# Another order, bank plan and loading of the first windows in a fused window-attention and Fourier kernel

## The chip, the cores and the metric

The kernel runs on one core of one Trainium2 chip. The metric is device time in microseconds (us) of one execution. The engines are TensorE (PE, which multiplies matrices and loads its weights ahead as PEld), VectorE (DVE), ScalarE (ACT), GpSimd (POOL) and SyncE (SP, which issues transfers here). Each engine works through its own queue in order. [...]

## The reference

There are 32 images of 56 x 56 positions and 128 channels, and two residual layers.

```python
x = x + window_attention(group_norm(x))   # 7x7 windows, shifted by 3, 4 heads of 32
x = x + fourier(group_norm(x))            # 32 groups of 4 channels in both norms

# window_attention, per window of 49 tokens
attn = q @ k.T * 32 ** -0.5 + bias + mask         # relative position bias, shift mask
out  = softmax(attn) @ v @ w_proj.T + b_proj

# fourier: the first 32 DCT modes along w and along h, mixed over channels, turned back, added
h   = idct(mix(dct(x, w)[:32], w0)) + idct(mix(dct(x, h)[:32], w1))
out = relu(h @ W1 + b1) @ W2 + b2                 # 128 -> 512 -> 128
```

## The kernel before, in words

All is computed in fp32. The work is written out in cycles by hand, with PE, ACT, DVE and POOL bound to the order of the program text (`manual_schedule`, L1073); SP's queue is ordered by the framework. Cycle r is one row of eight windows: image r // 8, row r % 8. A row passes through a pipeline of cycles:

- cycle r: `attn_qk` (L393): the products Q and K on PE, one bank each; ACT empties Q once and K twice, one time for each of two heads (L406, L416). `attn_scores` (L438): 16 products of K with Q into two banks (L451), emptied by DVE, which adds bias and mask `bm` (L459). `attn_max` (L466): DVE takes the maximum (L469), POOL subtracts it (L470). `attn_v` (L424): the product V (L429), copied by ACT (L436).
- the exponential on ACT (L476), the sum and its inverse on DVE (L481, L483), then POOL divides by multiplication in six pieces, into `blocks` (L495).
- cycle r + 2: DVE turns `blocks` (L505).
- cycle r + 3: `attn_values` (L508): probabilities times V into two banks (L520), emptied by ACT (L552) and DVE (L550). `attn_project` (L554): the output product, to which DVE adds the input with its bias, giving x (L569).
- cycle r + 4: sums of x and of its square over channels (L586, L593 on ACT, L594).

In the first eleven cycles (`CONV_BEGIN` is 11) `first_rows` (L1031) orders this: Q and K, the exponential of the row before, values, token bias on POOL, the division of the row before, turn, scores, maximum and subtraction, projection, steps of the norm of the next image, V. Two score buffers `a_sb` alternate. From cycle 11 on other functions (L894 to L1020) order it, and the Fourier layer of the image that is through runs beside the attention: statistics (`fourier_stats`, L608), transforms (L666), mixing (L700), going back (`modes_back`, L739, emptied by ACT L755 or DVE L750), and from cycle 19 the feed-forward in seven of eight cycles (`ff_in`, L759: four hidden blocks, each product into a bank, emptied by ACT at L776; `ff_out`, L790, emptied by DVE at L811). All `halved` products carry the line L110.

The banks are handed out in turn from two rings of four, and a product waits until the bank four places back in its ring has been emptied:

```python
def attn_bank(): return bank("pa", 4)   # Q, K, values, scores, V, projection, statistics, norm
def conv_bank(): return bank("pc", 4)   # transforms, mixing, modes, feed-forward
```

Loading and normalizing an image: its rows come in two halves k of 32 rows and two quarters u of each (`load_quarter`, L136), one buffer; DVE turns a quarter so that channels come on partitions (`turn_quarter`, L296: L308 to L319), takes statistics of each row (L329), and `image_norm` (L336) goes in steps from those to the power on POOL (rstd, L377), the scaled weights on ACT (wn, L385) and V's bias (L388, L389). Image 0 is loaded in two halves, four transfers each, from SP and ACT (L146). The relative position bias is set up by seven transfers of columns (L180), seven of rows (L184) and one copy (L187), the mask by four (L195), and `bias_and_mask` (L201) adds the two: for inner rows on DVE ahead of the cycles, for the last row of an image on POOL in cycles 4 and 5. POOL's memset in `mix_weights` (L244) precedes each load of a part of the mixing weights.

## Time and profile before

| | before |
|---|---|
| time, median of 3 runs | 3379.4 us (3378.18 to 3388.73) |
| time of the profiled execution | 3378.94 us |
| span in the profile | 3377.1 us |
| PE busy | 3252.4 us (96%) |
| weight loads (PEld) | 2561.5 us (76%) |
| DVE busy | 2468.8 us (73%) |
| POOL busy | 2334.6 us (69%) |
| ACT busy | 1979.1 us (59%) |
| moved by DMA | 448.85 MB, 133 GB/s on average |

The profile is one execution, as the hardware's profiler took it. Its page gives the busy time of each engine, its busy tenths in 40 equal slices of the span, and the clock that the throttle granted PE, in tenths. Views of the trace give busy time by stretches, the instructions in order of time (start, duration, engine, line, output <- inputs, and in brackets how long the engine had stood and what ended that), and who waited for whom. Ends of matmuls are modelled, since they are pipelined: rows overlap by a few tenths of a us.

### The profile page before, as it was taken

The page shows a single profiled execution, that of the slowest core. Times are in us where ns is not written, and L with a number is a line of the kernel's source. Part 1 is how long each engine was busy: PE and PEld are TensorE (multiplying, and loading weights), DVE is VectorE, ACT ScalarE, POOL GpSimd, SP SyncE. Part 2 cuts the span into 40 slices and gives each one's busy share as a digit, 9 for nine tenths or more (in the row PEclk, how much of TensorE's full clock was granted, in tenths as well). Part 3 has the DMA queues.
Part 4 walks back from the last instruction along what each step waited for, and adds up shares of the span by engine and source line. Part 5 has one row for each costly group of instructions (what it writes and reads, how often), then busy time and mean ns, then how long its engine had stood idle before and what let it go on. Part 6 is the DMA issues. An engine that isn't in the chain of part 4 may idle for free.

```text
span 3377.1 us, 158257 instructions
## 1 busy us (share of the span) xinstructions
PE 3252.4 (96%) x69504; PEld 2561.5 (76%) x69504; DVE 2468.8 (73%) x4793; ACT 1979.1 (59%) x3649; POOL 2334.6 (69%) x2724
## 2 busy tenths in 40 slices
PE   4689999999999999999999999999999999999999
PEld 2467777777878777777777777777777777777776
DVE  6778777777777777777778777777777778777641
ACT  2456665566655666666666665566665666665553
POOL 5777777677676777777777676677776777777641
PEclk8889999999999999999999999999999999999999
DMA  5546555556555555555556555555555655555443
GB/s 94 111 117 149 134 132 139 130 136 147 131 132 132 141 133 142 140 133 137 137 137 147 134 133 131 135 135 141 135 139 134 140 137 140 138 135 132 117 129 101
DMA packets 1158097, 448.85 MB, mean 133 GB/s; under 512 B 509951, under 2 KB 1127584, under 8 KB 1157408
## 3 DMA queue, kind: packets, MB, share of 16 engines
q1 hardware_dynamic: 1149565, 437.50, 54.2%
q8 instruction: 546, 8.95, 1.2%
q10 hardware_dynamic: 7843, 1.24, 0.3%
q14 instruction: 143, 1.17, 0.1%
HBM read 277.01 MB, written 161.48 MB: 130 GB/s over the span
## 4 chain that ended last, share of the span: by engine, by line
PE 78%; DVE 8%; POOL 5%; ACT 5%; issue 3%; DMA 1%; SPq 0%; DVEq 0%; POOLq 0%; ACTq 0%
PE pc L110 36%; PE pa L110 13%; PE pa L429 6%; PE pc L666 5%; PE pc L739 5%; PE pa L451 5%; PE pa L520 4%; PE pc L700 4%; POOL blocks L495 4%; ACT hid L776 2%; POOL a L470 1%; DVE eT L505 1%; DVE a L459 1%; DVE xw L308 1%; DVE st L329 1%
## 5 line engine op out<-in xcount | busy, mean ns | idle before, releaser
L495 POOL TENSOR_TENSOR blocks<-a,rs 32x512 f32<-32x512 f32 (+3 forms) x1536 | 1304.3, 856 | 646.9 <-DVE rs L483 542.4
L110 PE MATMUL pc<-wff,hid 128*64 128x128 f32 x12544 | 744.2, 273 | 2.5 <-issue 1.0
L110 PE MATMUL pc<-xf,wff 128*64 128x512 f32 (+2 forms) x3584 | 720.1, 539 | 1.1 <-DVE xf L750 0.9
L110 PEld LDWEIGHTS pc<-wff,hid 128*64 128x64 f32 x12544 | 705.0, 137 | 10.5 <-ACT hid L776 4.6
L110 PEld LDWEIGHTS pc<-xf,wff 128*64 128x64 f32 x3584 | 291.4, 136 | 344.1 <-issue 229.7
L470 POOL TENSOR_TENSOR a<-a,mx 128x784 f32<-128x784 f32 x256 | 386.0, 1508 | 235.4 <-DVE mx L469 202.5
L776 ACT ACTIVATE hid<-pc,b1sb 128x512 f32<-128x512 f32 (+2 forms) x896 | 512.9, 646 | 60.7 <-PE pc L110 52.6
L550 DVE TENSOR_SCALAR oT<-pa,bqkv 128x147 f32<-128x147 f32 (+2 forms) x768 | 171.1, 279 | 376.1 <-PE pa L520 376.1
L593 ACT ACTIVATE xr<-x 112x384 f32<-112x384 f32 (+1 forms) x256 | 147.1, 574 | 509.5 <-DVE x L569 509.5
L110 PE MATMUL pa<-xw,wn 128*64 128x392 f32 x2048 | 400.8, 500 | 41.3 <-ACT wn L385 36.2
L811 DVE TENSOR_TENSOR res<-pc,res 128x512 f32<-128x512 f32 (+3 forms) x257 | 143.0, 566 | 373.6 <-issue 168.3
L436 ACT COPY v<-pa 128x512 f32<-128x512 f32 x256 | 152.1, 594 | 356.4 <-PE pa L429 356.1
L783 POOL TENSOR_TENSOR res<-res,b2sb 128x512 f32<-128x512 f32 (+2 forms) x256 | 266.8, 1048 | 88.2 <-DMA res<-scr 88.2
L416 ACT ACTIVATE k<-pa,bqkv,heads 128x392 f32<-128x392 f32 x512 | 317.5, 673 | 2.3 <-PE pa L110 1.9
L476 ACT ACTIVATE a<-a 128x784 f32<-128x784 f32 x256 | 218.8, 855 | 170.4 <-POOL a L470 160.4
L505 DVE STREAM_TRANSPOSE eT<-blocks 128x1024 f32<-128x1024 f32 x256 | 315.7, 1233 | 0.0
L429 PE MATMUL pa<-wn,xw 128*64 128x128 f32 x4096 | 290.1, 283 | 15.9 <-issue 7.8
L124 POOL TENSOR_TENSOR xr<-xr,bproj 112x384 f32<-112x384 f32 (+1 forms) x256 | 292.5, 1142 | 7.4 <-DMA xr<-in_x_dram 7.3
L459 DVE TENSOR_TENSOR a<-pa,bm 128x392 f32<-128x392 f32 x512 | 265.2, 560 | 30.1 <-PE pa L451 6.5
L520 PEld LDWEIGHTS pa<-eT,v 49*32 49x32 f32 x16384 | 173.7, 106 | 146.5 <-issue 94.7
L110 PE MATMUL pa<-wproj,oT 128*48 128x128 f32 (+1 forms) x3584 | 253.3, 276 | 21.7 <-ACT oT L552 15.4
L481 DVE TENSOR_REDUCE sm<-a 128x16 f32<-128x784 f32 x256 | 245.2, 958 | 35.6 <-ACT a L476 35.5
(94 smaller groups left out, 5023.0 us busy)
## 6 DMA issues: line engine op xcount, KB each, us to landing
zscr<-z SPq DMA_DIRECT2D x512, 112.0 KB
xin<-in_x_dram SPq DMA_DIRECT2D x496, 112.0 KB
htok<-scr SPq DMA_DIRECT2D x256, 196.0 KB
zT<-zscr SPq DMA_DIRECT2D x192, 256.0 KB
res<-scr SPq DMA_DIRECT2D x160, 256.0 KB
out_dram<-res SPq DMA_DIRECT2D x160, 256.0 KB
scr<-x SPq DMA_DIRECT2D x128, 224.0 KB
xr<-in_x_dram SPq DMA_DIRECT2D x128, 168.0 KB
```

What stands on the lines that cost most here:

```text
L110: nc.tensor.matmul(dst[ps], lhsT=lhsT[:, ps], rhs=rhs, start=start, stop=stop)
L124: nc.gpsimd.tensor_tensor(piece, piece, bproj.unsqueeze(1).to_broadcast([TC, n, C]), ALU.add)
L416: nc.scalar.activation(k_sb[:, u], pk[:, :RT].rearrange("p (w j) -> p w j", j=WT), AF.Identity, bias=im.bias[:, 3 + u : 4 + u], scale=head ...
L429: nc.tensor.matmul(pv[HALVES[w % 2], w // 2 * C : (w // 2 + 1) * C], lhsT=im.half[i // NP][:, t0 : t0 + JP], rhs=im.w[:, 2 * C : 3 * C], s ...
L459: nc.vector.tensor_tensor(a[:, 2 * hp : 2 * hp + 2, :, 0:WT].rearrange("p u w j -> p w u j"), ps[hp][:, :RT].rearrange("p (w u j) -> p w u ...
L470: nc.gpsimd.tensor_tensor(a3, a3, mx.unsqueeze(2).to_broadcast([P, 2 * NWR, WT]), ALU.subtract)
L481: nc.vector.tensor_reduce(sm, a3, axis=AX.X, op=ALU.add)
L495: nc.gpsimd.tensor_tensor(dst[to, k, :, :n], a3[src, :, kb * KB : kb * KB + n], rs[src].unsqueeze(2).to_broadcast([src.stop - src.start, 2 ...
L505: nc.vector.transpose(eT.rearrange("p t (k j) -> p k t j", k=2), blocks[r % 2])
L520: nc.tensor.matmul(po4[u][h * HD : (h + 1) * HD, pr], lhsT=v[ks, pr, h * HD : (h + 1) * HD], rhs=eT[ks, h * NP + pr, :WT], start=True, sto ...
L776: nc.scalar.activation(hf[:, :n], ph[:, :n], AF.Relu, bias=b1sb[:, f : f + 1])
L783: nc.gpsimd.tensor_tensor(im.res[:m, c0:c1], im.res[:m, c0:c1], b2sb[:m].unsqueeze(1).to_broadcast([m, c1 - c0, C]), ALU.add,)
```

## The change

Seven things change together.

1. Banks: `pa` has two (Q, K, values, V). The scores have two banks of their own, `ps0` and `ps1`, zeroed once by DVE. The projection, V's bias and the statistics take banks of `pc`, which has four as before.
2. Scores: the weights are the 49 columns of a window and no longer 64, and only 49 of each 64 partitions are written. `q_sb` loses its padding.
3. The first rows use three score buffers, the third in a buffer of the transforms' y, which is free then.
4. In `first_rows` the values come ahead of the scores, as before, but scores, maximum, subtraction and exponential of a row now all stand ahead of the division of the row before.
5. Image 0 is loaded in quarters, 16 transfers of half the size, alternately from SP and ACT.
6. The 19 transfers of bias and mask are issued by POOL. The bias sums come behind the first norm on DVE, those of the last row in cycles 1 and 2 on DVE.
7. Two of the three norm steps of cycle 7 move to the end of cycle 6. The zeroing of the ends of xw goes from POOL to DVE.

```diff
     def attn_bank():
-        return bank("pa", 4)
+        return bank("pa", 2)
...
+    ps = [bank(f"ps{hp}", 1) for hp in range(2)]
+    for t in ps:
+        nc.vector.memset(t, 0.0)
...
-        pb = attn_bank()
+        pb = conv_bank()
...
-                        ps[hp][HALVES[e], pr * 2 * WT : (pr + 1) * 2 * WT],
-                        lhsT=q[cs, w * WT : w * WT + JP],
+                        ps[hp][e * JP : e * JP + WT, pr * 2 * WT : (pr + 1) * 2 * WT],
+                        lhsT=q[cs, w * WT : (w + 1) * WT],
...
-        pp = attn_bank()
+        pp = conv_bank()
...
-        pg = attn_bank()
+        pg = conv_bank()
...
+    def attn_buffer(r):
+        return a_sb[r % 3 if r < CONV_BEGIN - 2 else r % 2]
...
-            (nc.scalar if ix % 2 else nc.sync).dma_start(
+            nc.gpsimd.dma_start(
                 cols[ix : ix + 1].rearrange("p h y x -> p (h y) x"), src.unsqueeze(0)
             )
         for iy in range(WS):
-            nc.sync.dma_start(
+            nc.gpsimd.dma_start(
...
-    nc.sync.dma_start(rpb[JP : JP + WT], rpb[0:WT])
+    nc.gpsimd.dma_start(rpb[JP : JP + WT], rpb[0:WT])
...
-            nc.sync.dma_start(mask_sb[rows, :, k], src.rearrange("r p j -> p r j"))
+            nc.gpsimd.dma_start(mask_sb[rows, :, k], src.rearrange("r p j -> p r j"))
...
+            queue = nc.scalar if b == 0 and cb % 2 else nc.sync
+            queue.dma_start(t[cs], x[b, rows, u * HW : (u + 1) * HW, cs])
...
     def first_rows(cycle):
         im, i = row(cycle)
+        im3, i3 = row(cycle - 3)
         if im:
             attn_qk(im, i)
-        if cycle:
-            attn_exp(cycle - 1)
-        im3, i3 = row(cycle - 3)
         if im3:
             attn_values(im3, i3, cycle - 3)
         tokens_bias(cycle)
-        divide(cycle)
-        turn(cycle)
         if im:
             attn_scores(im, i, cycle)
             attn_max(cycle)
+            attn_exp(cycle)
+        divide(cycle)
+        turn(cycle)
         if im3:
             attn_project(im3, i3)
-        for _ in range(3 if cycle == NWR - 1 else cycle in (0, NWR)):
+        for _ in range(cycle in (0, NWR - 1, NWR)):
             norm_step(cycle)
...
-        if cycle in (4, 5):
+        if cycle in (1, 2):
             for half in range(2):
-                bias_and_mask(nc.gpsimd, 1, cycle - 4, half)
+                bias_and_mask(nc.vector, 1, cycle - 1, half)
         next_begin(cycle)
         next_groups(cycle)
+        if cycle == NWR - 2:
+            for _ in range(2):
+                norm_step(NWR - 1)
...
         if cycle == CONV_BEGIN - 1:
             attn_sums(im3, i3)
-            attn_exp(cycle)
...
+        extra = big.tile([P, NM * S + JP - S], F32, tag="y", name="a_extra", bufs=2)
+        extra = extra[:, : NH * NP * WT].rearrange("p (t w j) -> p t w j", t=NH, w=NP)
+        a_sb.append(extra)
```

More of the change, by code (lines that the diff above doesn't have):

```diff
@@ L128, in swin_fourier_kernel, with load_quarter @@
     HW = S // 2
-    def load_columns_of(dst, b, k, w0, w1, both=False):
+    def load_quarter(b, k, u):
+        if b:
+            t = work.tile([P, HW, KB], F32, tag="xin", name="xin", bufs=1)
+        elif u:
+            t = others[k]
+        else:
+            t = big.tile([P, NM * S + JP - S], F32, tag="y", name="xin_first", bufs=2)
+            t = t[:, : S * KB].rearrange("p (w c) -> p w c", w=S)
+            others.append(t[:, HW:])
+            t = t[:, :HW]
         rows = slice(k * (S - KB), k * (S - KB) + KB)
@@ L133, in load_columns_of @@
             cs = slice(cb * KB, (cb + 1) * KB)
-            (nc.scalar if both and cb % 2 else nc.sync).dma_start(dst[cs], x[b, rows, w0:w1, cs])
-    def load_quarter(b, k, u):
-        t = work.tile([P, HW, KB], F32, tag="xin", name="xin", bufs=1)
-        load_columns_of(t, b, k, u * HW, (u + 1) * HW)
+            queue = nc.scalar if b == 0 and cb % 2 else nc.sync
+            queue.dma_start(t[cs], x[b, rows, u * HW : (u + 1) * HW, cs])
         return t
-    xins = {}
+    xins, others = {}, []
     for k in range(2):
-        first = big.tile([P, NM * S + JP - S], F32, tag="y", name="xin_first", bufs=2)
-        first = first[:, : S * KB].rearrange("p (w c) -> p w c", w=S)
-        load_columns_of(first, 0, k, 0, S, True)
         for u in range(2):
-            xins[0, k, u] = first[:, u * HW : (u + 1) * HW]
+            xins[0, k, u] = load_quarter(0, k, u)
     x1 = big.tile([TC, NCH, C], F32, tag="x1", name="x1")
@@ L210, in bias_and_mask @@
                 )
-    for t in range(2):
-        for half in range(2):
-            bias_and_mask(nc.vector, 0, t, half)
     dct_w = const_load([TC, 2 * NM], dct, "dct_w")
@@ L271, in swin_fourier_kernel @@
         nc.vector.memset(heads[h * HD : (h + 1) * HD, h % 2 : h % 2 + 1], 1.0)
-    q_sb = big.tile([P, RT + JP - WT], F32, tag="q", name="q")
-    nc.gpsimd.memset(q_sb, 0.0)
+    q_sb = big.tile([P, RT], F32, tag="q", name="q")
     v_sb = [big.tile([P, NP, C], F32, tag=f"v{i}", name=f"v{i}") for i in range(3)]
     a_sb = [big.tile([P, NH, NP, WT], F32, tag=f"a{i}", name=f"a{i}") for i in range(2)]
+    def attn_buffer(r):
+        return a_sb[r % 3 if r < CONV_BEGIN - 2 else r % 2]
     blocks = [
@@ L302, in turn_quarter @@
             )
-            nc.gpsimd.memset(im.half[k][:, NWR * slot : NWR * slot + JP - WT], 0.0)
+            nc.vector.memset(im.half[k][:, NWR * slot : NWR * slot + JP - WT], 0.0)
         slots = im.half[k][:, : NWR * slot].rearrange("p (j h s) -> p s j h", j=NWR, s=WS)
@@ L438, in attn_scores @@
     def attn_scores(im, i, r):
-        q, a = q_sb, a_sb[r % 2]
-        ps = [attn_bank(), attn_bank()]
+        q, a = q_sb, attn_buffer(r)
         for pr in range(NP):
@@ L466, in attn_max @@
     def attn_max(r):
-        a3 = a_sb[r % 2].rearrange("p t w j -> p (t w) j")
+        a3 = attn_buffer(r).rearrange("p t w j -> p (t w) j")
         mx = small.tile([P, 2 * NWR], F32, tag="mx", name="mx")
@@ L474, in attn_exp @@
     def attn_exp(r):
-        a2 = a_sb[r % 2].rearrange("p t w j -> p (t w j)")
+        a2 = attn_buffer(r).rearrange("p t w j -> p (t w j)")
         nc.scalar.activation(a2, a2, AF.Exp)
     def attn_recip(r):
-        a3 = a_sb[r % 2].rearrange("p t w j -> p (t w) j")
+        a3 = attn_buffer(r).rearrange("p t w j -> p (t w) j")
         sm = small.tile([P, 2 * NWR], F32, tag="sm", name="sm")
@@ L486, in attn_divide @@
     def attn_divide(r, rs):
-        a3 = a_sb[r % 2].rearrange("p t w j -> p (t w) j")
+        a3 = attn_buffer(r).rearrange("p t w j -> p (t w) j")
         dst = blocks[r % 2]
@@ L1081, in swin_fourier_kernel @@
             norm_step(-1)
+        for t in range(2):
+            for half in range(2):
+                bias_and_mask(nc.vector, 0, t, half)
+        extra = big.tile([P, NM * S + JP - S], F32, tag="y", name="a_extra", bufs=2)
+        extra = extra[:, : NH * NP * WT].rearrange("p (t w j) -> p t w j", t=NH, w=NP)
+        a_sb.append(extra)
         for cycle in range(NB * NWR + CONV_BEGIN + FF_AT[-1] - NWR + 1):
```

## The prediction

> **What bounds the kernel now.** I read the page's busy lines and slices first, then busy time by stretches, then the order of time and the waits of three stretches: the first rows (0 to 149 us), the cycles before the feed-forward starts (149 to 235 us), and one later image.

> ```profile
> PE   4689999999999999999999999999999999999999
> PEclk8889999999999999999999999999999999999999
> ```

> A slice is 84.4 us. PE fills from the fourth slice on; only the first three have room.

> ```profile
> 100.00:120.00 20.00, 10.27 (x228) 6.34 (x224) 14.79 (x33) 7.78 (x16) 12.60 (x17) 0.80 0.44 71
> ...
> 2440.00:2840.00 400.00, 398.85 (x8648) 311.32 (x8644) 308.51 (x596) 245.97 (x456) 289.17 (x333) 1.00 0.57 137
> ```

> Columns: stretch, us, then busy us of PE, weight loads, DVE, ACT, POOL, the clock, the DMA share. Late in the run PE is busy 398.85 of 400 us at clock 1.00: there any wait put in front of PE is paid in full, and nothing that the other engines save is. From 0 to 240 us PE is busy 148 us, so 92 idle us are all that the change can win. In the first rows this chain sets the pace:

> ```profile
> 43.58 1.50 POOL L470 TENSOR_TENSOR a<-a,mx 128x784 f32<-128x784 f32 x1
> ...
> 45.11 0.86 ACT L476 ACTIVATE a<-a 128x784 f32<-128x784 f32 x1 [4.39 <-POOL a L470]
> ...
> 46.00 0.97 DVE L481 TENSOR_REDUCE sm<-a 128x16 f32<-128x784 f32 x1 [4.35 <-ACT a L476]
> ...
> 47.40 5.33 POOL L495 TENSOR_TENSOR blocks<-a,rs 128x512 f32<-128x512 f32 x6 [2.27 <-DVE rs L483]
> ...
> 52.81 1.50 POOL L470 TENSOR_TENSOR a<-a,mx 128x784 f32<-128x784 f32 x1
> ```

> Subtraction, exponential, sum, division, next subtraction: 52.81 - 43.58 = 9.23 us a cycle. The score additions (L459) of cycles 0 to 10 start at 31.39 and 133.93, so ten cycles take 102.54 us; two of them are long. Cycle 5 to 6 takes 14.27, with the load of a quarter waited for, and 7 to 8 takes 15.86, since the second image's scaled weights come last:

> ```profile
> 84.09 1.10 DVE L308 STREAM_TRANSPOSE xw<-xin 128x512 f32<-128x512 f32 x1 [4.38 <-DMA xin<-in_x_dram]
> ```

> ```profile
> 107.56 1.57 PE L110 MATMUL pa<-xw,wn 128*64 128x392 f32 x4 [6.83 <-ACT wn L385]
> ```

> **The change, part by part.** The sum is made against the profiled execution, 3378.94 us (span 3377.1 and 1.84 around it), 0.5 below the median of 3379.4. A cycle takes in one row of eight windows.

> *Start: +1 us.* Image 0 in quarters lets DVE's turns begin earlier. They began at 9.97, when 0.9 MB had landed, and DVE was then busy to 20.95. One quarter's turns (2.1 us) go ahead of that; the last quarter is still followed by turns, a copy and four statistics (2.0 + 0.2 + 2.0), so about 0.8 us is won. Against it, 19 small transfers go from SP and ACT to POOL: seven columns, four masks, seven rows, one copy, each kind waiting for an earlier one. They stand ahead of the power (rstd, L377, at 23.58), for which ACT's weights and PE wait. The trace has no transfer issued by POOL. Issued by SP the same ones took 1.18 each for columns (4.70 for 4), 0.45 (masks), 0.83 (rows), 0.80: 16.7 in all, and the copy landed 3.4 us after its issue began. From 2.1 (the memset of bm) that gives columns to 10.4, masks to 13, rows to 19, landing, copy at 22.2: hidden. At the dearest issue in the trace, 2.07 each (8.27 for four quarters' loads), 19 take 39 us and the power comes some 19 us late. I take +1, near the transfers' own rows, and keep -1 to +19. The bias sums on DVE (16 at 0.18) end by 29, two us ahead of the first scores. [...]

> *First rows: -3 us.* With the subtraction ahead of the division the 9.23 us chain is cut: exponential and sum lie beside the division. POOL then needs 1.50 + 5.33 + 1.13 (token bias) + 0.4 = 8.4. But a longer loop takes its place, since the exponential of a cycle now stands in ACT's queue ahead of the copy of V, the bank of that copy is the one that the next product for K needs (two banks left), and the product of probabilities and V needs K's bank: subtraction 1.50, exponential 0.86, square 0.56, copy of V 0.58, product K 0.78, evictions 1.25, values 0.95, scores 0.90, additions 1.00, maximum 0.97, less some 0.2 of overlap and with handovers of 0.05: 9.5. So an ordinary cycle gains nothing. The first two have no values and no square: 8.0 each; the third and fourth 9.0. Cycle 5 to 6: the sums of biases leave POOL, so the weights' memset and the quarter's load behind it on SP come earlier; DVE's own work (10.6) and the landing leave 11.4. Cycle 7 to 8: two steps of the norm go ahead; the weights are ready, and mean products and their evictions add 0.9 to 10.1: 11.0. Sum 8 + 8 + 9 + 9 + 10 + 11.4 + 9.5 + 11 + 9.5 + 9.5 = 94.9, 7.6 less. At the end POOL has two divisions to make one after the other: from the additions of cycle 10 to the end of its division, 2.0 (additions, maximum) + 1.5 + 5.4 + 1.4 (sums, token bias) + 5.4 = 15.7, where 147.62 - 133.93 = 13.7 were taken; 5.6 of the gain is left. The clock takes part of it: PE now stands 2.1 to 3.1 us in front of product K, on the loop. In this trace a stop of 2.06 us (at 176.29) was followed by scores of 1.58 instead of 0.90, one of 1.77 (122.75) by full speed. That is 1.4 us a cycle, 0 to 14 in all; I take 2.6. Bounds -7 to +9. [...]

> *Cycles 11 to 18: +7 us.* With four banks the values could run while ACT was still evicting K; with two they stand behind it. Cycle 17 of before:

> ```profile
> 210.23 0.92 PE L520 MATMUL pa<-eT,v 49*32 49x49 f32 x62 [1.90 <-DVE x L569]
> ...
> 211.08 2.52 PE L739 MATMUL pc<-idcth,zT 64*64 64x112 f32 x48
> ...
> 211.22 1.24 ACT L416 ACTIVATE k<-pa,bqkv,heads 128x392 f32<-128x392 f32 x2
> ...
> 213.37 1.10 PE L451 MATMUL pa<-k,q 64*64 64x98 f32 x32
> ...
> 214.52 0.57 DVE L459 TENSOR_TENSOR a<-pa,bm 128x392 f32<-128x392 f32 x1 [1.48 <-PE pa L451]
> ```

> Values began at 210.23 as soon as x was out; K's evictions ended at 212.46. Values, the modes and the scores behind them on PE go 2.2 later, and DVE was waiting for those scores. About +2.0 here, +2.05 in cycle 18 (values 220.06, K out 222.17). In cycle 14 the scores waited for K anyway (178.46); values now stand between: +0.85. In cycle 11 V's product waited for DVE (149.16); its bank will be the one that ACT empties behind four copies of y (151.24): +2.1. The wait of values for x (5.9 us in three cycles) goes, but x is ahead of K in ACT's queue (square, Q, K), so K is late next. Bounds 0 to +8.

> *All later images: +10 us.* PE is the bound. Banks of the scores and the bank of the projection change no wait there: K is out 0.09 to 1.9 us ahead of the values in every cycle that I read. But the statistics of image b (L613) take a bank of the feed-forward's four, right behind the four hidden blocks, so the bank of the first, which ACT must have emptied:

> ```profile
> 431.45 1.24 ACT L416 ACTIVATE k<-pa,bqkv,heads 128x392 f32<-128x392 f32 x2
> ...
> 432.57 2.43 ACT L776 ACTIVATE hid<-pc,b1sb 128x512 f32<-128x512 f32 x4
> 432.69 0.29 PE L110 MATMUL pa<-tot,gmean 112*64 112x64 f32 x4
> ```

> The first of the four blocks is out at 432.57 + 0.65 = 433.22, PE is there at 432.69: 0.55 of waiting. Over 30 images this time is 0.45 to 0.57 in 18, and 0 to 0.3 in the rest: 10.5 us. Bounds 0 to 11. The lone wait of values in the cycle without feed-forward has 0.09 to spare: up to 1.5, in the bounds.

> *Narrower score weights: -1.* 49 columns instead of 64. The scores take 0.72 us from start to start in a late image, and their moving columns are the same; weight loads of 64 columns (137 ns) and of 32 (106) bound it at 0 to -5. PE's stops for no visible reason (L429, L666, L739; 22 us between 340 and 3200) may fall elsewhere: -6 to +6.

> Sum: 1 - 3 + 7 + 10.5 - 1 = +14.5, so **3393 us**.

> **The rivals.** *Faster, 0.15:* POOL becomes the bound of the first rows. If the copy of V is out early, so that product K follows product Q at once, ten cycles are 8.4 to 11 each, 87 us instead of 102.5; with 2 lost at the end, start -1, and the later waits covered (ACT a little earlier than before), that is some -15: 3364. For it: the 9.23 us chain is really cut. Against it: ACT's order puts the copy behind the exponential in every cycle. It decides from the point where the loop through ACT falls under 8.4.

> *No change, 0.20:* the wait of the statistics is hidden because their own input is late as well (DVE's part ends at 432.70). Then +4: 3383.

> *Much slower, 0.10:* POOL's transfers cost 2.07 each and hold the power: +18 on top, 3411. For it: 19 issues in one queue, four links of waiting. Against: POOL has stood idle from 4.6 to 23.6.

> *The forecast, 0.55:* 3385 to 3403, with the terms above; some four fifths of it lie above 3389.

> **The numbers.** 0.3% is 10 us, about what a measurement of this kernel can tell from no change; its borders are 3369 and 3389. Slower: 0.44 of the forecast and the 0.10 of the transfers, 0.54. Faster: 0.15, and 0.01 from the low end of the second case. Within: 0.11 of the forecast and 0.19, 0.30. The range leaves out about half of the faster case and half of the slowest: 3366 to 3408.

> **What would show it.** In the profile after: ordinary first cycles of 9 to 10 us with PE's second product waiting for the copy of V; no wait of PE for wn near cycle 8; a wait for K ahead of the values in cycles 14, 17 and 18; a wait of about 0.5 us at the product of tot, once an image; the power within 2 us of 23.6. First cycles of 8.4 us, or no wait at tot, would make the forecast wrong.

## The result and the profile after

| | before | after |
|---|---|---|
| time, median of 6 runs each, same chip | 3379.76 us (3374.62 to 3388.73) | 3423.75 us (3417.15 to 3433.5) |
| after / before | | 1.0129, 95% interval 1.0109 to 1.0148 |
| span of the profiled execution | 3377.1 us | 3431.7 us |
| PE busy | 3252.4 us | 3273.1 us |

The change costs 44 us. The forecast had the sign, but 13 of 44 us, and the time lies above its range (3366 to 3408). The profiled execution of after is the slowest of its six: its span is 54.6 us longer, so some 10 of what the traces compare below are scatter. Two of six runs of the kernel with the bank part alone, and one of six of the kernel with the statistics' sums in a scores' bank, took 7.6 to 9.5 ms; the times given for these two are medians of their other runs.

First the slices of the page, then two of the stretches shown of before (same columns):

```profile
PE   4679999999999999999999999999999999999999
PEclk8789999999999999999999999999999999999999
```

```profile
2440.00:2840.00 400.00, 386.44 (x8369) 301.43 (x8367) 294.90 (x579) 236.45 (x438) 279.61 (x318) 1.00 0.55 133
100.00:120.00 20.00, 14.54 (x270) 10.96 (x272) 15.14 (x36) 7.50 (x16) 14.73 (x22) 0.67 0.54 106
```

The slices look alike. The stretches do not: late in the run PE is busy 386.44 of 400 us where it was busy 398.85, at clock 1.00, and from 100 to 120 us its clock is 0.67 where it was 0.80.

**Where the time goes.** I compared the start of the same instruction in both traces. After starts its first score additions 0.9 us earlier (30.52). At cycle 10 it is 2.9 us late, at cycle 11 4.8, at the first product of `tot` of image 1 (242.95 against 231.30) 11.7, and from there it loses on, to 54 at image 30: some 43 us in the later images.

**The first rows** run in the loop that the forecast described. One cycle in order of time:

```profile
96.95 1.50 POOL L476 TENSOR_TENSOR a<-a,mx 128x784 f32<-128x784 f32 x1 [2.62 <-DVE mx L475]
...
98.49 0.86 ACT L482 ACTIVATE a<-a 128x784 f32<-128x784 f32 x1 [4.72 <-POOL a L476]
...
99.66 0.57 ACT L443 COPY v<-pa 128x512 f32<-128x512 f32 x1
...
100.28 0.89 PE L110 MATMUL pa<-xw,wn 128*64 128x392 f32 x4 [2.13 <-ACT v L443]
...
102.58 0.80 PE L526 MATMUL pa<-eT,v 49*32 49x49 f32 x62 [1.21 <-ACT k L423]
...
103.30 1.56 PE L457 MATMUL ps<-k,q 64*49 64x98 f32 x32
```

The exponential (L482) waits for the subtraction, the copy of V (L443) stands behind it, PE's product for K waits 2.13 us for that copy's bank, and the values wait for K's eviction. The scores then take 1.56 us instead of 0.90: PE is cold, by which I mean the granted clock, 0.50 from 103.30 to 104.80 where it was 1.00 at K's product (100.28 to 101.17). Cycles take 9.6, 9.6, 11.1, 9.5, 9.4, 15.1, 10.7, 11.5, 9.5, 10.4, in all 106.3.

**The later images.** What PE waited for between 340 and 3200 us (total us, times, longest), after first, then before:

```profile
PE pc L745 <- issue: 22.8, 18, 2.2
PE pc L672 <- issue: 14.5, 16, 2.1
PE pa L436 <- issue: 9.4, 10, 1.5
PE pc L110 <- POOL blocks L501: 7.4, 15, 0.5
PE pc L110 <- issue: 1.9, 4, 0.6
```

```profile
PE pc L666 <- issue: 8.2, 14, 1.1
PE pa L429 <- issue: 7.8, 10, 1.6
PE pc L739 <- issue: 6.1, 7, 1.4
...
PE pc L110 <- issue: 1.0, 3, 0.4
```

The fourth line of after is the wait at `tot` that the forecast named; in order of time:

```profile
446.62 2.43 ACT L782 ACTIVATE hid<-pc,b1sb 128x512 f32<-128x512 f32 x4
...
447.45 0.34 PE L110 MATMUL pc<-tot,gmean 112*64 112x64 f32 x4 [0.49 <-POOL blocks L501]
```

The first of the four hidden blocks is out at 446.62 + 0.65 = 447.27, and `tot` follows; the view names POOL, whose event came at about the same time, but the bank is ACT's. That is 7.4 us. The rest is "issue": stops in which PE waited for nothing that the profile shows. They grow from 23.1 to 48.6 us.

**What an "issue" stop is.** Part 3 of the page of after (queue, kind: packets, MB, share) has a queue that moves instructions:

```profile
q8 instruction: 546, 8.95, 1.2%
```

```profile
1373.21 0.34 PE L110 MATMUL pc<-tot,gmean 112*64 112x64 f32 x4 [0.54 <-POOL blocks L501]
...
1373.59 0.81 PE L526 MATMUL pa<-eT,v 49*32 49x49 f32 x64
1374.33 0.89 PE L457 MATMUL ps<-k,q 64*49 64x98 f32 x32
1375.04 0.93 PE L745 MATMUL pc<-idctw,zT 64*64 64x112 f32 x28
1377.92 0.79 PE L745 MATMUL pc<-idctw,zT 64*64 64x112 f32 x20 [1.95 <-issue]
```

The packet with the next piece starts at 1375.41, takes 0.88 us, and PE goes on 1.63 us after its end. Over the 82 borders of before that come under 5 us behind the one ahead and at which PE goes on within 1.9 us of the packet's end, the packet starts 1.5 us after PE has crossed the border ahead (median), takes 1.1, and is used 1.5 later: 4.1 us for a piece. More than half of the pieces last PE 5 to 9 us (267 of 481 of before between 340 and 3200 us), and nothing shows. But from `tot` on PE has 64 products for the values, 32 for the scores and 48 for the modes, in the trace each with a weight load of its own: a whole piece in 2.4 us.

An image has 4373 instructions in before and 4370 in after, 17 pieces and 21 or 18 more. So the borders move through the program from image to image and are back after 12 to 14: before's images take 100.2 us where the borders fall into sparse stretches and up to 103.4 where they fall behind the dense ones.

### The profile page after: what moved, and what is told of

The parts are those of the page before. It is cut to its first block, busy times and chain, and to the rows that moved or that the text cites. A ratio compares the mean times of both kernels' runs of the same rounds, so it can differ in the third digit from the quotient of the medians.

```text
span 3431.7 us, 158187 instructions
## 1 busy us (share of the span) xinstructions
PE 3273.1 (95%) x69504; PEld 2565.1 (75%) x69504; DVE 2481.5 (72%) x4875; ACT 1978.7 (58%) x3649; POOL 2335.5 (68%) x2662
## 3 DMA queue, kind: packets, MB, share of 16 engines
q10 hardware_dynamic: 7712, 1.24, 0.3%
## 4 chain that ended last, share of the span: by engine, by line
PE 73%; DVE 9%; POOL 6%; ACT 5%; issue 5%; DMA 2%; POOLq 0%; DVEq 0%; ACTq 0%; SPq 0%
PE pc L110 36%; PE pa L110 7%; PE pa L436 6%; PE pc L745 5%; PE pc L672 5%; PE ps L457 5%; PE pa L526 4%; PE pc L706 4%; POOL blocks L501 4%; ACT hid L782 2%; ACT k L423 1%; POOL a L476 1%; DVE sm L487 1%; DVE a L465 1%; DVE eT L511 1%
## 5 line engine op out<-in xcount | busy, mean ns | idle before, releaser
L501 POOL TENSOR_TENSOR blocks<-a,rs 128x512 f32<-128x512 f32 x1518 | 1288.9, 856 | 658.1 <-DVE rs L489 555.4
L110 PE MATMUL pc<-wff,hid 128*64 128x128 f32 x12544 | 743.5, 273 | 3.2 <-issue 1.9
L110 PE MATMUL pc<-xf,wff 128*64 128x512 f32 (+2 forms) x3584 | 719.8, 539 | 1.1 <-DVE xf L756 0.9
L110 PEld LDWEIGHTS pc<-wff,hid 128*64 128x64 f32 x12544 | 704.7, 137 | 10.9 <-ACT hid L782 4.6
L476 POOL TENSOR_TENSOR a<-a,mx 128x784 f32<-128x784 f32 x253 | 381.4, 1508 | 281.2 <-DVE mx L475 260.7
L110 PEld LDWEIGHTS pc<-xf,wff 128*64 128x64 f32 x3584 | 288.8, 136 | 346.8 <-issue 220.4
L110 PE MATMUL pa<-xw,wn 128*64 128x392 f32 x2048 | 406.0, 504 | 53.4 <-ACT wn L392 30.3
L443 ACT COPY v<-pa 128x512 f32<-128x512 f32 x256 | 151.6, 592 | 368.8 <-PE pa L436 368.7
L482 ACT ACTIVATE a<-a 128x784 f32<-128x784 f32 x253 | 216.1, 854 | 175.5 <-POOL a L476 174.9
L124 POOL TENSOR_TENSOR xr<-xr,bproj 112x384 f32<-112x384 f32 (+1 forms) x256 | 291.9, 1140 | 11.7 <-DMA xr<-in_x_dram 11.5
L465 DVE TENSOR_TENSOR a<-ps,bm 128x392 f32<-128x392 f32 x506 | 262.2, 560 | 41.1 <-PE ps L457 19.2
L436 PEld LDWEIGHTS pa<-wn,xw 128*64 128x64 f32 x4096 | 228.5, 140 | 55.4 <-issue 14.9
L110 PE MATMUL pc<-wproj,oT 128*64 128x128 f32 (+1 forms) x3584 | 254.3, 277 | 3.0 <-issue 1.3
```

The costliest lines, as they stand in the source:

```text
L110: nc.tensor.matmul(dst[ps], lhsT=lhsT[:, ps], rhs=rhs, start=start, stop=stop)
L124: nc.gpsimd.tensor_tensor(piece, piece, bproj.unsqueeze(1).to_broadcast([TC, n, C]), ALU.add)
L436: nc.tensor.matmul(pv[HALVES[w % 2], w // 2 * C : (w // 2 + 1) * C], lhsT=im.half[i // NP][:, t0 : t0 + JP], rhs=im.w[:, 2 * C : 3 * C], s ...
L465: nc.vector.tensor_tensor(a[:, 2 * hp : 2 * hp + 2, :, 0:WT].rearrange("p u w j -> p w u j"), ps[hp][:, :RT].rearrange("p (w u j) -> p w u ...
L476: nc.gpsimd.tensor_tensor(a3, a3, mx.unsqueeze(2).to_broadcast([P, 2 * NWR, WT]), ALU.subtract)
L482: nc.scalar.activation(a2, a2, AF.Exp)
```

## The experiments

The kernel before ran beside each on the same chip. Ratios are to it, with 95% intervals. Theory A and B are defined in the first text.

**The parts alone.** The diff was split in three: banks; order and buffers of the first rows; start.

> The kernel before with the bank part alone: two banks for the products, two own banks for the scores, 49-column weights, and projection, statistics and the bias of V in the feed-forward's four. Theory A (PE takes its instructions in pieces of 256, the next piece is only asked for around the crossing into the last one, and a wait at the products of tot holds that request up): all of the loss of the later images comes with this part, some +32, and the start's cycles give 0 to +10 on top: 3410 to 3422 us. Theory B (the forecast's terms were right, the rest of the loss comes from the new order of the first rows or is scatter): +7 and +10.5 on 3379.8: 3390 to 3398.

3434.97 us, 1.0155 (1.0139 to 1.0172): the bank part alone costs 52 us, more than the whole change, more than the 30 to 42 us of theory A and far more than the 10 to 18 of theory B. At image 1 it is 11.5 us late.

> The kernel before with the new order of the first rows alone (three score buffers, exponential ahead of division, norm steps earlier), four banks and the old start. Theory A: the later images keep before's periods, and with four banks the product for K needs no copy of V, so cycles fall from 9.2 towards the 8.4 us that POOL needs: 3365 to 3378 us. Theory B, by which the order brings part of the loss: 3385 or more.

3377.16 us, 0.9984 (0.9975 to 0.9994). Ten cycles take 94.3 us, and image 1 comes 8.4 us earlier. With four banks the product for K has a bank that is long empty. So with four banks the order gains 8.4 us there and 5.7 of the whole time, about half of what the "faster" rival asked for, and two banks take it away again: alone they cost 11.5 up to image 1, with the order's 8.4 and the start's 1.1 taken off that would be 2.0, but after is 11.7 late.

> The kernel before with the new start alone (image 0 in quarters, small transfers from POOL, sums of biases on DVE). Both theories: first additions 0.9 us earlier, cycles 1 and 2 longer by 8 sums of biases on DVE, cycles 4 and 5 relieved of them on POOL: 3374 to 3381 us.

3382.43 us, 0.9998 (0.9989 to 1.0008): nothing that can be measured, where a gain of up to 6 was expected.

**The loop through ScalarE.** In after, the exponential of a cycle goes behind its V:

```diff
             attn_max(cycle)
-            attn_exp(cycle)
...
             attn_v(im, i, cycle)
+            attn_exp(cycle)
```

> The changed kernel with the exponential of the first rows behind the copy of V in ScalarE's queue, in its own cycle; the rest as changed. If the loop through ScalarE sets the first rows, as the forecast says, the second product no longer stands behind the exponential: cycles of 9.5 become 8.4 to 9, the additions of cycle 10 start some 8 to 12 us ahead of 136.8, and the time falls to 3410 to 3418 us. If something else sets them (TensorE's cold products, VectorE), the time stays at 3420 to 3428.

3417.83 us, 1.0101 (1.0085 to 1.0118); the additions of cycle 10 start at 127.41, 9.4 us earlier than in after, and ten cycles take 97.4 and not 106.3. So the loop through ScalarE did set most of the first rows. The whole time falls by 6 us, and its interval touches that of after (1.0109 to 1.0148).

**The statistics' bank**, undone in after and done alone in before:

```diff
-        pg = conv_bank()            # after
+        pg = ps[0][:, RT:]          # spare columns of a scores' bank
...
-        pg = attn_bank()            # before
+        pg = conv_bank()
```

> The changed kernel with the sums of the statistics in spare columns of a scores' bank, so that they need none of the feed-forward's four; the rest as changed. Theory A: the 0.5 us wait at the products of tot goes in 17 images (7 us) and with it the late requests for the next piece, so that the stops of PE in the 300 instructions behind tot fall from some 34 us to some 14: 3424 - 7 - 20 = 3397, 3390 to 3404 us. Theory B: only the wait itself goes: 3414 to 3419.

3406.21 us, 1.0064 (1.0048 to 1.0080): 17.5 us less than after, or 22 by the two ratios to before, which were taken apart. That is more than theory B's 5 to 10 and just short of theory A's range. No wait at `tot` is left, and the "issue" stops between 340 and 3200 us fall from 48.6 to 37.3.

> The kernel before with one line changed: the statistics' sums in one of the feed-forward's four banks. Theory A (the wait at the products of tot costs twice, once by itself and once as the request for the next piece of instructions stands behind it): 17 x 0.5 for the wait and 10 to 15 for longer stops in the instructions behind tot: 3400, 3394 to 3408 us. Theory B (only the wait): 3387 to 3393.

3408.40 us, 1.0068 (1.0052 to 1.0083): one line costs before 26 us, as theory A said, just above its range. What PE waited for between 340 and 3200 us:

```profile
PE pc L666 <- issue: 14.8, 19, 1.6
PE pc L739 <- issue: 14.3, 10, 2.5
PE pc L110 <- POOL blocks L495: 9.7, 18, 0.5
```

18 waits of half a us are 9.7; beside them the "issue" stops rise from 23.1 to 37.1, at the products right behind `tot` (L739, L666). So the wait ahead of this dense run costs more than its own length, and the packets show how. Take the borders that lie from one weight load ahead of `tot` to 15 behind it. There before asks for the next piece 1.2 to 3.2 us ahead of PE's crossing (four borders), this kernel, one line away from it, 1.3 to 2.2 us after the crossing (four), and after 1.8 to 2.1 us after it (three).

> The kernel before with one line changed: the projection in one of the feed-forward's four banks. Theory A (the rest of the loss of the later images comes from two banks, since values that wait for K hold the request for instructions up): no loss here, 3379 to 3386 us. Rival: the projection's place in the feed-forward's ring brings the rest: 3390 or more.

3379.18 us, 0.9992 (0.9982 to 1.0001): the projection in the feed-forward's ring costs nothing that can be measured.

**Is it the supply of instructions?** First the borders are moved:

```diff
+        dummy = attn_bank()
+        for _ in range(32):
+            nc.tensor.matmul(dummy[: P // 2, :1], lhsT=gmean[:, : P // 2], rhs=gmean[:, :1], start=True, stop=True)
```

> The kernel before with 32 products of one column ahead of the first image, 128 instructions, half a piece; nothing else. Theory A: the time stays within 8 us of 3380, but the long images (102 and more: images 5 to 10 and 18 to 22 in the traced run of before) come 128/21 = 6 images earlier or later: around images 11 to 16 and 24 to 28. Theory B: they stay where they were.

3383.93 us in one run. Images of 102 us and more were 5 to 8, 10, 18, 20 to 22 and 30 in before; here they are 2 to 4, 11 to 15, 25, 26 and 28. Nothing that the engines compute for an image had changed. The 32 products move the borders, and by taking one bank they move all later banks of their ring by one place, in every image alike. The long images moved as the borders did, which ties the stops to them.

Then the borders are held in place, by products on all 128 columns in place of two halves (one of three such lines):

```diff
-                halved(p[:, RT : RT + 1], w, im.mean)
+                nc.tensor.matmul(p[:, RT : RT + 1], lhsT=w, rhs=im.mean, start=True, stop=True)
```

> The kernel before with the five small products of an image (bias of Q, K and V, two for the statistics) on all 128 columns at once and not in halves: 20 instructions of PE fewer an image, 4353 instead of 4373 (17 pieces of 256 are 4352). The place of an image in the pieces then moves by 1 an image and not by 21, and stays where the traced run of before had its short images (100.2 to 101.0 us). Theory A (the stops come from the supply of instructions): nearly all later images take 100.2 to 101.0, 3380 - 26 = 3354, 3345 to 3362 us. Theory B (the stops come from data, transfers or scatter): long images remain in the same rhythm, 3374 to 3382.

3404.72 us, 1.0059 (1.0043 to 1.0076): a miss by 50. The rhythm is gone, as theory A said, and "issue" stops fall a little (19.2 us), but the shortest images take 101.1 us and no longer 100.2. The products themselves cost that: from `tot` to the values alone it is 0.59 us instead of 0.33 with halves, and all five make some 0.9 us an image (an estimate, 101.1 less 100.2), 28 in all, which I had set at nothing. And the place was not as good as thought, since more than half of the images still had a stop at L739.

> The same with 36 products of one column put ahead of the first image, where PE stands idle: 144 instructions, which move every image to the place where the traced run of before had its long images. Theory A: nearly all later images take 102 to 103.5, 3380 + 38 = 3418, 3400 to 3430 us. Theory B: as the kernel without them, 3374 to 3382.

3474.47 us, 1.0264 (1.0244 to 1.0283). The same program with 144 instructions ahead of it takes 70 us longer. Both kernels lie some 50 us above theory A's numbers, but the difference between them that it asked for, 3418 - 3354 = 64, was there. Waits between 340 and 3200 us:

```profile
PE pc L666 <- issue: 36.3, 39, 2.6
PE pa L429 <- issue: 27.3, 40, 1.4
```

With 1.1 at L739 these are 64.7 us of "issue" stops where its twin has 19.2. The place of the borders makes that difference. The stops are 45 of the 70 us; the page also has PE busy for 3316.0 us instead of 3289.2, and why the products take longer is not shown.

> The changed kernel with the same five small products on all 128 columns, 4351 instructions of PE an image, and 24 products of one column ahead of the first image, so that its images stay where the traced run after had its short ones. The wait at the products of tot is kept. Theory A: images of 100.7 to 101.4 instead of 102.9 on average, 3424 - 50 = 3374, 3362 to 3385 us. Theory B: 3415 to 3428.

3429.84 us, 1.0135 (1.0120 to 1.0150), not 3374. The stops fell as theory A asked (from 48.6 to 20.5), but the products on 128 columns took some 0.9 x 30 = 27 back (the figure of the kernel made from before), and the wait at `tot` rose from 7.4 to 13.9, as it now came in 27 images. The three make 6 us, which was measured: as a test of theory A through the time it failed, through the stops it held.

**The rest of the later loss** (r2 explains 26 of some 32 in before, but after without the wait at `tot` still has 37.3 us of stops): with two banks the values can't start ahead of K's eviction. That wait alone was put into before. The narrower weights and the scores' own banks have no run of their own:

```diff
+            e = im.eT[i][0:1, 0, 0:1]     # from cycle 25 on
+            nc.scalar.copy(e, e)          # behind K | behind Q | behind the exponential before
```

> The kernel before with one addition from cycle 25 on: ScalarE copies one element of the turned probabilities onto itself right behind the evictions of K, so that the values can't start ahead of K, as with two banks; banks, order and start are before's. Theory A (a wait at the head of a dense run holds up the request for the next piece of instructions even where it costs little by itself): some 10 to 17 us over the kernel before, 3390 to 3400. Rival (the rest of the later loss has another source than the values' wait): 3380 to 3387, and the same as its control.

3403.68 us, 1.0060 (1.0047 to 1.0072). That is above theory A's range. PE waited for this copy twice in all, 0.4 us, and yet:

```profile
PE pc L739 <- issue: 17.5, 16, 2.0
PE pc L666 <- issue: 13.8, 17, 2.1
PE pa L429 <- issue: 9.9, 14, 1.8
...
PE pa L520 <- ACT eT L898: 0.4, 2, 0.2
```

> The control of the kernel whose values wait for K: the same copy of one element, ahead of the evictions of K in ScalarE's queue and behind that of Q, so that the values wait for it but it is out 1.2 us earlier. Theory A: less than half of the other's loss, 3380 to 3388 us. If the copy itself were what costs: the same as the other one.

3401.27 us, 1.0051 (1.0038 to 1.0063): a miss, 18 us over before and not under 8. The copy was out 0.9 to 3.1 us ahead of the values here, 0.05 to 1.9 above.

> A second control of the kernel whose values wait for K: the same copy of one element, right behind the exponential of the cycle before, ahead of square, Q and K in ScalarE's queue, so that it should be out 3 us and more ahead of the values. Theory A (a wait met within the last 3 us holds the request for instructions up, one met earlier does not): within 5 us of the kernel before, 3379 to 3388. If the copy, or one more wait among PE's instructions, is what costs: 3398 to 3406 as the other two.

3396.20 us, 1.0037 (1.0024 to 1.0051): 13 us, again more than the 5 expected, with the copy out 1.6 to 7.3 us ahead (3 to 3.5 in three of eight cycles). The earlier the wait is met the less it costs, 21, 18, 13, but no point was reached at which it costs nothing. The packets point to a reason. At the borders that were named with the statistics' bank, between 340 and 3200 us, before and the six kernels with such borders that add no wait there ask for the next piece 0.9 to 3.2 us ahead of the crossing (23 borders). After and the seven kernels that do add one ask 0.9 to 2.6 us after it (27 borders), and this one too (1.6 to 2.5), though behind `tot` its copy is out 3.4 us and more ahead of the values. So one more wait among PE's instructions goes with a late request even when it is met early. How the 13 to 21 us split stays open: the copies also change PE's count for an image from 4373 to 4368, 4376 and 4375, so these images lie at other places of the pieces than before's.

**A version that beats both.** The order of the first rows with the old banks, and no bias of K; then with its borders moved by 54 products of one column (one of the lines that leave out the bias):

```diff
-            if i == 0:
+            if i == 0 and part == 0:
                 halved(p[:, RT : RT + 1], w, im.mean)
```

> The new order of the first rows with the old banks and the old start, and without the bias of K: it adds the same number to all scores of a query, which the softmax takes out again, so its product (8 instructions of PE and some 0.39 us an image) and its scaling are left out. Both theories: 3377 - 31 x 0.39 = 3365, 3358 to 3370 us.

3360.65 us, 0.9931 (0.9916 to 0.9947), as expected.

> The kernel with the new order of the first rows, the old banks and no bias of K, and 54 products of one column ahead of the first image, where PE stands idle: 216 instructions, which put image 1 on place 184 of a piece instead of 224 (it moves by 13 an image). Theory A: ten images lie on the places with long images instead of some 13.6, 2 us each: 3361 - 7 = 3354, 3349 to 3359 us. Theory B: 3359 to 3363.

3356.68 us, 0.9917 (0.9904 to 0.9931). The "issue" stops are 16.9 us instead of 20.7, and the time lies in theory A's range, but the intervals of the two ratios overlap: that a better place was won is not shown by the time.

## Why the prediction was right or wrong

- **Start, +1:** nothing measurable alone. The transfers from POOL were cheap: seven columns in 3.83 us. The power came at 22.80 (23.58 before).
- **First rows, -3:** wrong, +5.6 up to the additions of cycle 11 in the trace (4.8 late, after a start 0.9 early). The mechanism was right: K's product waited for the copy of V, and moving the exponential took 9.4 us out. The end was right too: 1.9 lost behind cycle 10, 2 forecast. The sizes were not. Ten cycles took 106.3 and not 94.9 + 2.6. 3.7 of that is cycle 5 to 6, where POOL's token bias stood 5.5 us for its load, ahead of the subtraction, which I had not priced. 3.2 are the first two cycles, 9.6 and not 8.0: K's product took 1.58 us and the scores 1.56, where I had 0.78 and 0.90. In the second of them the granted clock was 0.51 at K's product (45.17) and 0.50 at the scores (48.14); in the first (35.55 and 38.54) the view gives 1.00 for the same lengths, so what made them is not shown there. Another 2.1 are cycle 2 to 3, 11.1 and not 9.0, whose additions stood behind eight sums of biases on DVE that took 4.5 us and not 1.4. And PE was cold in later cycles too (its granted clock was 0.67 to 0.84 in stretches of 20 us between 40 and 180 us, in before 0.67 to 0.91), while I had taken 2.6 of a range of 0 to 14.
- **Cycles 11 to 18, +7:** right in sum: 4.8 late at cycle 11, 11.7 at image 1. Not in its places: cycles 11 and 14 lost nothing, 17 and 18 lost 5.4 instead of 4.05, the rest came behind them.
- **Later images, +10.5:** the step that failed. The wait at `tot` is there, 0.5 us in 17 images, 7.4 us between 340 and 3200. But I priced it by its own length. With it, ahead of the densest run of an image, the request for the next piece comes 1.3 to 2.2 us after the crossing in the kernel with this one line changed, where before's comes 1.2 to 3.2 us ahead, and the bank costs 17 to 22 us in after and 26 in before. "Banks of the scores and the bank of the projection change no wait there" was true of the waits and false of the time: with a wait put in front of the values, met 0.05 to 1.9 us ahead, before lost 21 us, though PE stood there for 0.4 us in all. How much of the loss of after comes by this path is not measured: its later images still lose some 15 us in the trace without the wait at `tot`.
- **Narrower score weights, -1:** within its bounds (0 to -5), as far as the traces show; no run has them alone. From start to start the scores take 0.715 us where they took 0.728 (medians of 200 rows between 340 and 3200 us), some 3 us over 256 rows.
- **PE's stops for no visible reason, -6 to +6:** +25.5 in the trace. I took them for scatter that falls here or there. Nearly all of those over 0.3 us lie at the borders of the pieces (37 of 38 in before, 50 of 55 in after), whose packets the profile before held in its queue of instructions (q8, 546), and the change acted on them.
- **The rivals:** "no change" fell, as `tot` did wait. "Much slower" came nearest to the time (3411) by luck: its reason, a late power, did not come. "Faster" described in kind what the order does with four banks, at about half its size.

## What to carry to other kernels

Where PE is the bound, count its instructions as well as its time. Here, where pieces were short, the next one was used 4.1 us after the border ahead (median of before). Behind `tot`, before used up a piece of 256 in 2.1 to 3.0 us and did not stop at its end, with the next one's packet 1.2 to 3.2 us ahead of the crossing (four borders); after, with the packet 1.8 to 2.1 us behind it, stopped there for 1.7 to 2.2 us (three). A wait put in front of such a run cost more than its length: 26 us with 9.7 of waiting, and 21 where PE stood for 0.4. An "issue" stop that repeats at the same instruction number modulo 256, as 87 of 93 did here, points to this. Try a new order and a new bank plan apart: here the one gained 6 us, and the other took them back and 44 more.

## What the runs showed of the hardware that I had not expected

- Where pieces are short, the packet with the next piece of PE's instructions starts 1.5 us after the crossing of a border, and the piece is used 4.1 us after it (medians of 82 such borders of before; 4.1 of about a hundred of after). In image 12 of after PE crosses a border at 1373.32, the packet starts at 1375.41, and its piece is the one that PE goes on with at the next border, at 1377.92.
- Two halves of a small product are cheaper here than one on 128 columns: the statistics' products take 0.33 us up to the values, in one piece 0.59 (the kernel with five such products on all 128 columns).
- Beside POOL's division, sums of biases on DVE took 0.56 us each on average (4.46 for eight, from 43.25 in after) and not 0.18, and the division itself 5.64 and not 5.33.
- A small transfer issued by POOL took 0.55 us of its queue (columns, 3.83 for seven in after), where SP took 1.18 (4.70 for four in before).
